# A mixture of experts in an order planned on the host: first gate products by single token blocks, one load queue at the start, and an order planned anew with shorter lengths

## The chip, the cores and the metric

The kernel runs on one core of a Trainium2 chip. The core's engines are TensorE (PE; its weight loads are listed apart as PEld), VectorE (DVE), ScalarE (ACT), GpSimd (POOL) and SyncE (SP), each with its own queue of instructions that it works off in order. The metric is the device time of one execution in microseconds (us); lower is better. All arithmetic is in float32.

## The reference

The input x has 16 batch entries of 256 tokens with 256 features. Eight routed experts and one shared expert each have an up part (two matrices of 256 x 1024, the gate G and the up matrix U) and a down matrix of 1024 x 256:

```python
g = einsum('bsd,edf->ebsf', h, Wg)
u = einsum('bsd,edf->ebsf', h, Wu)
expert_outs = einsum('ebsf,efd->ebsd', silu(g) * u, Wd)
expert_output = einsum('be,ebsd->bsd', gating_probs, expert_outs)
shared = einsum('bsf,fd->bsd', silu(h @ Sg) * (h @ Su), Sd)
x = x + (1 - sg) * expert_output + sg * shared      # h = x, sg per batch entry
```

## The kernel before

**Units.** The work is cut into 72 units: 9 experts x 2 halves of the 1024 hidden columns x 4 groups of four batch entries. A unit multiplies 512 hidden columns (four chunks of 128) with four token blocks of 256 tokens. Most units save matmuls by a fast algorithm: weights and tokens are combined at the points -1, 0, 1, 2, four diagonal products go to the one PSUM bank called D, and six pairs of points (PAIRS) give off-diagonal products in banks called M and X. The combined tokens are the tiles xd (diagonal) and xp (pairs), the combined weights wb and wp. The combined tokens of each group are made once, kept in DRAM (keep) and loaded again for later experts (load_xd, load_xp).

**Three stages.** Units 4 to 55 are "star" units: their down part also works in pairs (unit_up, unit_down), and their results are summed in DRAM as star totals. Units 1 to 3 and 56 to 71 use another form of the down part (unit_up_w, unit_down_w). At the passages between these, SBUF regions change their use (plan.shift, with the RANK entries "to" and "back"), and after unit 56 the star totals of the four groups are merged into the other totals (merge, RANK entries m0, m1, pace, ml).

**Unit 0** is computed plainly, since no combined tokens exist yet. Token blocks are loaded, transposed on TensorE (L560), and copied to SBUF by ACT (L565) as a raw pair of blocks. Eight steps (a, c), for pair a of blocks and chunk c, each have a product for the gate (m = 0, into an X bank) and one for the up matrix (m = 1, into an M bank). Each product is two matmuls of 512 columns, one for each half of the 256 features; the lower half of the weights comes from load_base, the upper half from load_raw. Before the first load lands, nine matmuls on zeros run.

**The queues of the first loads.** SP issues token block 0, block 1, the raw upper half of Wg, the lower half of Wu, then blocks 2 and 3. ACT issues two loads at the same time: the lower half of Wg and the raw upper half of Wu.

**What sets the order.** Every operation is added to a Plan with a rank, a length and a lag (HOP) until its result can be used. One rank step is a twelfth of a unit. Plan.run goes through time as these lengths say: whenever an engine is free, it takes the ready operation of the lowest rank plus "ahead" (TensorE keeps rank order in each of two streams: the dn bank's and the others), if its buffers are free. Operations of VectorE and POOL on SBUF alone (port) are booked one after another. The order that comes out is the fixed order of each engine's queue; waits between engines are by semaphore. So lengths and ranks are never executed, but decide the order. In a star unit, a diagonal goes: two matmuls into D, ACT's copy of D to a p tile (L673, rank entry "p"), two more matmuls into D, VectorE's subtraction (into pq, "q", "qa"), then ACT's SiLU of D for the gate (L874, with "ga" as its "ahead") or VectorE's product for the up part. Only then is D free for the next diagonal. ACT also scales the SiLU's result (L865) and moves down results from dn banks to ev tiles (L1103, L1026). POOL makes the differences s from p and q (L365), VectorE adds them to M to seed X (L365), and POOL combines weights. The file's helpers tt and stt record most VectorE and POOL operations, so these show lines L365 and L370; TensorE's products show L646, loads L360.

Of the kernel before, what the change touches and what calls it, by code (L numbers as in the profile page):

```python
# [16 lines left out]
P = 128  # L17
TB = 256
# [4 lines left out]


RANK = {
# [5 lines left out]
    (-15, -6, -33, -13, -49), "back": (36, 81, -9, -33, -38, 74, 23),  # L31
}


# [29 lines left out]
class Plan:  # L64
# [8 lines left out]

    HOP = 0.25
    KB = 0.0035

    def __init__(self):
# [124 lines left out]
def kernel(  # L204
# [42 lines left out]
    W = 12  # L247
# [63 lines left out]
    MM = 0.431  # L311
    TR = 0.16

    def dve(n, stt=False):
        return (0.2 if stt else 0.12) + n * 0.00112

    def act(n):
        return 0.24 + n * 0.0007

    def pool(n):  # L320
        return 0.43 + n * 0.00183 if n < 4 * P else 1.365

    ident = const.tile([P, P], F32, tag="ident", name="ident")
    make_identity(nc, ident)
# [57 lines left out]
    def load_base(m, e, half, rank, ranks=None):  # L382
        b = Buf("wb", f"wb_{m}_{e}_{half}")
        src = [
            sources(e)[m][ts(part, P), ts(half, 4 * P)].rearrange("p (c q) -> p c q", q=P)
            for part in range(2)
        ] if m < 2 else None
        late = 0 if rank < 0 else 8
        ru, rv = ranks or (rank, rank)
        if m == 2:  # L390
            rows = sources(e)[2][ts(half, 4 * P), :].rearrange("(c p) (k q) -> p c k q", p=P, q=P)
        engine = "ACT" if ranks and m == 0 else "SP"
        if m == 2:
            u = v = load(ru, lambda: b.tile, rows, 512, [], [b], late=late)
        else:
            u = load(ru, lambda: b[:, :, 0, :], src[0], 256, [], [b], late=late, engine=engine)
            v = load(rv, lambda: b[:, :, 1, :], src[1], 256, [], [], [b], late=late)
        ops = []
        for i, t in enumerate(POINTS):
            r, x_ = (lambda i=i: b[:, i, 1, :]), (lambda i=i: b[:, i, 0, :])  # L400
            if t == 0:
                op = v
            elif abs(t) == 1:
                op = tt("POOL", rank + 1, r, r, x_, ALU.add if t > 0 else ALU.subtract, P, [u, v], uses=[b])
            elif e == half == 0:
                op = stt(rank + 1, r, x_, float(t), r, ALU.add, P, [u, v], uses=[b])
            else:
                twice = Buf("wp", f"twice_{m}_{e}_{half}")
# [34 lines left out]
    def load_raw(ranks):  # L443

        b = Buf("wb", "wb_raw")
        ops = [
            load(
                ranks[m], lambda m=m: b[:, :, m, :],
                sources(0)[m][ts(1, P), 0 : 4 * P].rearrange("p (c q) -> p c q", q=P), 256,
                [], [b] if m == 0 else [], [b] if m else [], engine=("SP", "ACT")[m],  # L450
            )
            for m in range(2)
        ]
        return b, ops
# [88 lines left out]

    raw = {}

    def make_raw(a, rank, load_rank):

        b = Buf("pq", f"raw_{a}")
        done = []
        for n in range(2):  # L550
            i = 2 * a + n
            xin = Buf("xio", f"xin_0_{i}")
            src = x[i].rearrange("(h p) d -> p h d", p=P)
            ld = load(load_rank, lambda xin=xin: xin[:, :, :], src, 256, [], [xin])
            pt = Buf("dn", f"xt_0_{i}")

            def transposes(pt=pt, xin=xin):
                for k in range(2):
                    for h in range(2):
                        nc.tensor.transpose(pt[:, k, ts(h, P)], xin[:, h, ts(k, P)], ident)  # L560

            tr = add("PE", 4 * TR, rank, transposes, [ld], [pt], [xin])

            def copy(n=n, pt=pt):
                nc.scalar.copy(b[:, n : n + 3 : 2, :], pt[:, :, :])  # L565

            done.append(
                add(
                    "ACT", act(2 * TB), rank, copy, [tr],
                    [b] if n == 0 else [], [pt] if n == 0 else [pt, b],  # L570
                )
            )
        raw[a] = (b, done)
# [65 lines left out]
    def star(n):  # L639

        return FIRST <= n < LAST
# [54 lines left out]
    def offdiagonal(n, unit, k, rank, pqs, pqops, consume):  # L696

        e, half, g = unit
        i, j = PAIRS[k]
        xb, xo = xp[g, k], xpop[g, k]  # L700
        mb = Buf("M", f"M_{n}_{k}")
        m1 = []
# [8 lines left out]
        for m in range(2):  # L711
            w, wo = pair[m, e, half, k], pairop[m, e, half, k]
            p_, q_ = pqs[m]
            s, xbank = Buf("s", f"s_{m}_{n}_{k}"), Buf("X", f"X_{m}_{n}_{k}")
            so = tt(
                "POOL", rank + m - (RANK["s"] if star(n) else RANK["ws"]), lambda s=s: s[:, :, :], lambda q_=q_: q_[:, i : j + 1 : j - i, :],
                lambda p_=p_: p_[:, 3 - j : 4 - i : j - i, :], ALU.subtract, 2 * TB, [pqops[m][i], pqops[m][j]],
                [s], [p_, q_],
            )
            seed = tt(  # L720
                "DVE", rank + m + (RANK["seed"] if star(n) else RANK["wseed"]), lambda xbank=xbank: xbank[:, :, :],
                lambda m=m: mb[:, m : m + 1, :].broadcast_to([P, 2, TB]), lambda s=s: s[:, :, :], ALU.add, 2 * TB,
                [so, *m1], [xbank], [mb, s], False,
            )
            m67 = [
                mm(
                    MM, rank + m + (LAGX if star(n) else RANK["lagw"]) + (3 + h) / 8, lambda xbank=xbank, h=h: xbank[:, h, :],
                    lambda w=w, h=h: w[:, 2 - h, :], lambda h=h: xb[:, 2 - h, :],
                    False, True, True, [seed, wo, xo[2 - h]], [], [xbank, w, xb],
                )  # L730
                for h in range(2)
            ]
            consume[m](xbank, m67, rank + m + (LAGX + RANK["xc"] if star(n) else RANK["lagw"] + RANK["wxc"]), [(j, i), (i, j)])
# [35 lines left out]
    def unit_up_w(n, unit):  # L769
        e, half, g = unit  # L770
        r0 = W * n
# [39 lines left out]
        if n == 0:  # L811
            w, wops = first_raw
            readers = {0: [], 1: []}
            for step, (a, c) in enumerate((a, c) for a in range(2) for c in range(4)):
                xb, xo = raw[a]
                for m in range(2):
# [4 lines left out]
                    def view(k, xb=xb):  # L821
                        return xb.tile[:, 2 * k : 2 * k + 2, :]

                    m0 = mm(
                        2 * MM, r, lambda bank=bank: bank[:, :, :], lambda b0=b0, c=c: b0[:, c, 0, :],
                        lambda view=view: view(0), True, False, False, [u, *xo], [bank], [b0, xb],
# [5 lines left out]
                    readers[a].append(m1)  # L832
                    (gate, mult)[m](f"p{step}")(bank, [m1], r + 0.6, [(c, 2 * a), (c, 2 * a + 1)])
            for a in range(2):
                sum_raw(a, 8 + a, readers[a])
            return hb, hops

        pqs = {m: (Buf("pq", f"p_{m}_{n}"), Buf("pq", f"q_{m}_{n}")) for m in range(2)}
# [14 lines left out]
    def unit_up(n, unit):  # L853
# [7 lines left out]

        def scale(b, h, block, rank, deps):
            return add(
                "ACT", act(TB), rank,
                lambda: nc.scalar.mul(b[:, h, :], b[:, h, :], coef[:, e, 4 * g + block : 4 * g + block + 1]),  # L865
                [*deps, coef_op], uses=[b],
            )
# [475 lines left out]
    for n, unit in enumerate(units):  # L1343
        e, half, g = unit
        r0 = W * n
        if n == 0:
            make_raw(0, -14, -20)
            load_base(0, e, half, -16, (-20, -16))
            first_raw = load_raw((-19, -17.5))
            load_base(1, e, half, -15, (-18, -15))  # L1350
            make_raw(1, -5.5, -17)
        elif g == 0:
            for m in range(2):
                load_base(m, e, half, r0 - W + 3 * m - 8)
# [11 lines left out]
            rows = load_rows(e, half, r0 - 2)  # L1366
        if n == 1:
            for a in range(2):
                make_xd(g, a, -3.4 + 2 * a, -14, -3 + 2 * a)
            for k in range(len(PAIRS)):  # L1370
                make_xp(g, k, 5 + k)
            for a in range(2):
                make_xd(2, a, 3.2 + 2 * a, -13, 5 + 2 * a)
            for k in range(len(PAIRS)):
                make_xp(2, k, 11 + k / 2, True)
        elif n == 3:
            for a in range(2):
                make_xd(g, a, r0 - W + 6 * a - 4, r0 - W + 6 * a - 6, r0 - W + 6 * a - 7)
            for k in range(len(PAIRS)):
                make_xp(g, k, r0 + 2 * k - 5)  # L1380
        elif n == 4:
            for a in range(2):
                load_xd(g, a, r0 - W + 6 * a - 4)
# [101 lines left out]
```

## Time and profile before

| What | Value |
|---|---|
| Median of 3 runs | 2498.42 us (2497.76 to 2498.76) |
| The profiled execution | 2496.74 us |
| Its span, first to last instruction | 2495.0 us |
| Instructions | 34958 |
| TensorE's granted clock | 1.00 |
| DMA | 525.09 MB, mean 210 GB/s |
| VectorE 512 columns, X from M and s | 693 ns each, 632 times |
| POOL 512 columns, s from pq and pq | 1352 ns each, 852 times |
| ACT scaling of 256 columns (L865) | 509 ns each, 832 times |
| ACT eviction of a dn bank (L1103) to ev | 588 ns each, 456 times |

How to read it: a row of a group gives the line, the engine, the operation, the tile it writes and those it reads, the shape, how often, and then the busy time, the mean duration and the idle time of the engine just before. Durations are from start to end; the next operation of the same engine may start before the end of the last, so that a row's mean is longer than what one costs in a row of many. A matmul in float32 appears as two records. Times in the timeline count from the start of the span.

### The profile page before, as it was taken

The numbers are of one execution on the slowest core, as the hardware profiler recorded it, in microseconds if no ns is written. First come the engines' busy times: TensorE is split into PE (matmuls) and PEld (weight loads), VectorE is DVE, ScalarE is ACT, GpSimd is POOL, SyncE is SP. The second block draws the span as 40 slices with busy tenths as digits, with TensorE's granted clock in tenths as the row PEclk, the third lists the DMA queues.
The fourth block names the chain that finished last, engine by engine and source line by source line (L and its number), as shares of the span: only waits on it lengthen the run. The fifth ranks groups of instructions, "written<-read, shape, count | busy, mean of one in ns | idle before, by whom it ended". The sixth has DMA issues, their size and how long they took to land.

```text
span 2495.0 us, 34958 instructions
## 1 busy us (share of the span) xinstructions
PE 2473.5 (99%) x10886; PEld 2052.9 (82%) x10886; DVE 1867.7 (75%) x3142; ACT 1622.1 (65%) x3373; POOL 1807.4 (72%) x1947
## 2 busy tenths in 40 slices
PE   9999999999999999999999999999999999999999
PEld 5768888888888888888888888888888777777777
DVE  5787777777777777777777777777777888887787
ACT  3357777777777777787777778777777333333331
POOL 6777776768686868677776868586866788677764
PEclk9999999999999999999999999999999999999999
DMA  7546679888898888889988889888888888687776
GB/s 252 177 144 213 226 209 225 207 215 212 221 219 216 210 205 219 209 220 215 224 206 216 209 222 217 214 210 204 217 209 224 247 213 201 189 188 217 168 205 206
DMA packets 195770, 525.09 MB, mean 210 GB/s; under 512 B 16864, under 2 KB 83440, under 8 KB 186112
## 3 DMA queue, kind: packets, MB, share of 16 engines
q0 software_dynamic: 39552, 214.52, 44.6%
q1 hardware_dynamic: 154976, 307.81, 36.8%
q8 instruction: 87, 1.43, 0.2%
q14 instruction: 99, 0.81, 0.1%
q10 hardware_dynamic: 1056, 0.52, 0.1%
HBM read 290.53 MB, written 232.26 MB: 210 GB/s over the span
## 4 chain that ended last, share of the span: by engine, by line
PE 96%; DVE 2%; issue 1%; ACT 1%; DMA 0%; DVEq 0%; SPq 0%; ACTq 0%
PE dn L646 31%; PE M L646 22%; PE X L646 22%; PE D L646 19%; DVE h L365 1%; DVE X L365 0%; DVE pq L365 0%; PE dn L1291 0%; DVE big L370 0%; DVE h L370 0%; PE dn L522 0%; DMA side<-in_x_dram 0%; ACT sg L874 0%; DVE big L365 0%; ACT ev L1103 0%
## 5 line engine op out<-in xcount | busy, mean ns | idle before, releaser
L365 POOL TENSOR_TENSOR s<-pq,pq 128x512 f32<-128x512 f32 x852 | 1134.6, 1352 | 463.5 <-DVE X L365 233.8
L365 DVE TENSOR_TENSOR X<-M,s 128x512 f32<-128x512 f32 x632 | 427.1, 693 | 189.3 <-PE M L646 122.6
L646 PE MATMUL M<-xp,wp 128*128 128x256 f32 x1992 | 512.0, 379 | 1.9 <-DVE M L365 1.9
L646 PE MATMUL X<-xp,wp 128*128 128x256 f32 x1944 | 507.6, 379 | 1.5 <-DVE X L365 1.4
L646 PEld LDWEIGHTS M<-xp,wp 128*128 128x128 f32 x1992 | 378.1, 190 | 79.9 <-issue 25.6
L646 PE MATMUL D<-xd,wb 128*128 128x256 f32 x1696 | 436.9, 380 | 6.7 <-ACT sg L786 4.0
L646 PEld LDWEIGHTS X<-xp,wp 128*128 128x128 f32 x1944 | 368.8, 190 | 88.0 <-issue 34.8
L865 ACT ACTIVATE sg<-sg,coef 128x256 f32<-128x256 f32 x832 | 391.3, 509 | 1.2
L646 PEld LDWEIGHTS D<-xd,wb 128*128 128x128 f32 x1696 | 320.8, 190 | 75.0 <-issue 18.6
L1103 ACT COPY ev<-dn 128x512 f32<-128x512 f32 x456 | 267.4, 588 | 160.6 <-PE dn L646 157.2
L365 DVE TENSOR_TENSOR X<-X,sg 128x512 f32<-128x512 f32 x242 | 168.4, 696 | 172.1 <-ACT sg L865 109.1
L901 DVE TENSOR_TENSOR big<-big,X 128x1024 f32<-128x1024 f32 x242 | 292.6, 1209 | 0.0
L365 DVE TENSOR_TENSOR pq<-D,pq 128x256 f32<-128x256 f32 x568 | 229.4, 416 | 77.3 <-PE D L646 73.0
L646 PE MATMUL dn<-h,wp 128*128 128x256 f32 x1036 | 272.7, 379 | 0.3 <-ACT ev L1103 0.3
L673 ACT COPY pq<-D 128x512 f32<-128x512 f32 x284 | 166.5, 586 | 131.5 <-PE D L646 124.6
L646 PEld LDWEIGHTS dn<-h,wp 128*128 128x128 f32 x1036 | 196.6, 190 | 28.5 <-ACT ev L1103 0.7
L646 PE MATMUL dn<-h,low 128*128 128x512 f32 (+1 forms) x522 | 211.6, 507 | 0.0
L365 DVE TENSOR_TENSOR M<-M,s 128x512 f32<-128x512 f32 x220 | 152.5, 693 | 64.7 <-PE M L646 38.3
L1103 ACT COPY big<-dn 128x512 f32<-128x512 f32 x220 | 129.2, 587 | 77.5 <-PE dn L646 75.8
L874 ACT ACTIVATE sg<-X 128x512 f32<-128x512 f32 x224 | 134.1, 599 | 68.6 <-PE X L646 65.5
L1026 ACT COPY ev<-dn 128x512 f32<-128x512 f32 x122 | 71.4, 587 | 161.1 <-PE dn L646 159.5
L1117 POOL DMA_DIRECT2D star<-ev x130 | 113.6, 874 | 65.2 <-ACT ev L1103 51.4
(171 smaller groups left out, 3955.8 us busy)
## 6 DMA issues: line engine op xcount, KB each, us to landing
xp<-keep_p SPq DMA_DIRECT2D x408, 384.0 KB, 5.1
star<-ev POOLq DMA_DIRECT2D x104, 768.0 KB, 7.5
xd<-keep_d SPq DMA_DIRECT2D x136, 512.0 KB, 3.9
star<-big POOLq DMA_DIRECT2D x52, 768.0 KB, 7.6
star<-ev POOLq DMA_DIRECT2D x36, 1024.0 KB, 11.6
total<-ev POOLq DMA_DIRECT2D x17, 1024.0 KB, 8.6
star<-big POOLq DMA_DIRECT2D x16, 1024.0 KB, 11.3
total<-ev POOLq DMA_DIRECT2D x18, 768.0 KB, 7.6
```

The lines of the kernel that those rows point to most:

```text
L365: return add(engine, length, rank, lambda: eng.tensor_tensor(o(), a(), b(), op), deps, new, uses, port=port)
L646: lambda: nc.tensor.matmul(o(), w(), mv(), start=start, stop=stop, skip_group_check=onto),
L673: lambda: nc.scalar.copy(p_[:, 2 - 2 * a : 4 - 2 * a, :], bank[:, :, :]), ps,
L865: lambda: nc.scalar.mul(b[:, h, :], b[:, h, :], coef[:, e, 4 * g + block : 4 * g + block + 1]),
L874: lambda: nc.scalar.activation(b[:, :, :], bank[:, :, :], AF.Silu), deps, [b], [bank],
L901: "DVE", dve(4 * TB), rank, lambda: nc.vector.tensor_tensor(view(), view(), twice(), ALU.add),
L1026: lambda ev=ev, at=at, bank=bank: nc.scalar.copy(ev[:, at, :], bank.tile.rearrange("p a t -> p (a t)")),
L1103: lambda ev=ev, at=at, bank=bank: nc.scalar.copy(ev[:, at, :], bank.tile.rearrange("p a t -> p (a t)")),
L1117: nc.gpsimd.dma_start(star_total[g][part], ev[:, 0:k, :], accum_op=ALU.add)
```

## The change

Three things change in the program, and with them the order of nearly everything.

**Unit 0's first gate products.** For m = 0 and steps 0 and 1, the two matmuls of 512 columns become four of 256: first both halves of the features for block 0 (h = 0), then the same for block 1 (h = 1). Their ranks are -7 + h/5 + step/20. Each block's product depends on that block's copy alone. make_raw takes a rank for each block; block 1's transposes go to -6.97, between the two steps' products for block 0.

**One load queue at first.** The two loads issued by ACT go to SP. SP's order is then block 0, lower Wg, raw upper Wg, block 1, lower Wu, raw upper Wu, blocks 2 and 3, and the rest.

**Lengths and ranks.** The plan's lengths for VectorE, ACT and POOL become shorter, HOP longer (0.3 for 0.25); POOL's s operation in star units keeps 1.365, and the scaling by ACT is given 0.44 for 0.42. Most entries of RANK have new values, and seven ranks that were numbers in the code become entries (hX, hA, hR, hD, hE, hF, hG).

```diff
-    "first": 4, "q": 2.85, "dc": 2.95, "acc": 3.05, "g": -5.35, "cp": 1.1, "seed": -0.8, "s": 0.75,
-    "lagx": 1.0, "sc": 16.6, "bank": (6.6, 7.1, 8.6, 15.9, 16.4, 16.9, 17.3), "ev": 0.3, "p": 0.3, "xc":
-    0.2, "st": 1.7, "qa": -2.0, "da": -1.5, "ga": -4.75, "pace": 4, "m0": 0.4, "m1": 3.25, "xm": 0, "w":
-    16, "mp": 4, "m2": 1.5, "ml": 2.75, "lagw": 1.25, "wp": -0.2, "wq": 0.35, "wqa": -2.5, "wdc": 0.7,
-    "ws": 1.5, "wseed": 0.2, "wxc": 1.2, "pa": -3.5, "hd": (), "ph": 7.0, "pd": 0.75, "xh": 5.25, "to":
-    (-15, -6, -33, -13, -49), "back": (36, 81, -9, -33, -38, 74, 23),
+    "first": 4, "q": 2.85, "dc": 2.45, "acc": 2.55, "g": -5.35, "cp": 1.85, "seed": -0.3, "s": 0.75,
+    "lagx": 1.0, "sc": 15.85, "bank": (6.6, 7.1, 8.6, 15.9, 16.4, 16.9, 17.3), "ev": 0.3, "p": 2.3,
+    "xc": 0.2, "st": 1.2, "qa": -2.0, "da": -1.25, "ga": -7.25, "pace": 2, "m0": 1.9, "m1": 2.5, "xm":
+    0, "w": 16, "mp": 4, "m2": 1.5, "ml": 1.75, "lagw": 1.0, "wp": -0.95, "wq": -0.9, "wqa": -2.25,
+    "wdc": 2.2, "ws": 0.5, "wseed": 0.2, "wxc": 0.95, "pa": -4.25, "hd": (), "ph": 7.25, "pd": 1.0,
+    "xh": 5, "hX": 4.5, "hA": 10.5, "hR": 5.0, "hD": -6.5, "hE": 5, "hF": -7.75, "hG": -3.75, "to":
+    (-18, -3, -9, -16, -46), "back": (-27, 120, 21, -15, -5, 80, 20),
...
-    HOP = 0.25
+    HOP = 0.3
...
-        return (0.2 if stt else 0.12) + n * 0.00112
+        return (0.15 if stt else 0.09) + n * 0.00106
...
-        return 0.24 + n * 0.0007
+        return 0.21 + n * 0.000625
...
-        return 0.43 + n * 0.00183 if n < 4 * P else 1.365
+        return 0.38 + n * 0.00188 if n < 4 * P else 1.28
...
-        engine = "ACT" if ranks and m == 0 else "SP"
...
-                [], [b] if m == 0 else [], [b] if m else [], engine=("SP", "ACT")[m],
+                [], [b] if m == 0 else [], [b] if m else [],
...
+            if star(n):
+                so.length = 1.365
...
+                    if m == 0 and step < 2:
+
+                        m1 = None
+                        for h in range(2):
+                            rh = -7 + h / 5 + step / 20
+                            for k, (wv, wo) in enumerate(
+                                ((lambda b0=b0, c=c: b0[:, c, 0, :], u), (lambda c=c: w[:, c, 0, :], wops[0]))
+                            ):
+                                m1 = mm(
+                                    MM, rh + k / 100, lambda bank=bank, h=h: bank[:, h, :], wv,
+                                    lambda xb=xb, k=k, h=h: xb.tile[:, 2 * k + h, :], h == k == 0, k == 1, h == 1,
+                                    [wo, xo[h], m1], [bank] if h == k == 0 else [],
+                                    [w if k else b0, xb] if h == k == 0 else [w if k else b0, xb, bank],
+                                )
+                        readers[a].append(m1)
+                        gate(f"p{step}")(bank, [m1], r + 0.6, [(c, 2 * a), (c, 2 * a + 1)])
+                        continue
...
-                sum_raw(a, 8 + a, readers[a])
+                sum_raw(a, RANK["hR"] + a, readers[a])
...
-                "ACT", act(TB), rank,
+                "ACT", 0.44, rank,
...
-            make_raw(0, -14, -20)
-            load_base(0, e, half, -16, (-20, -16))
-            first_raw = load_raw((-19, -17.5))
+            make_raw(0, (-14, -6.97), (-20, -18.6))
+            load_base(0, e, half, -16, (-19, -16))
+            first_raw = load_raw((-18.8, -17.5))
             load_base(1, e, half, -15, (-18, -15))
-            make_raw(1, -5.5, -17)
+            make_raw(1, (-5.5, -5.5), (-17, -17))
...
-                make_xd(g, a, -3.4 + 2 * a, -14, -3 + 2 * a)
+                make_xd(g, a, -3.4 + 2 * a, -14, RANK["hD"] + 2 * a)
...
-                make_xp(g, k, 5 + k)
+                make_xp(g, k, RANK["hX"] + k)
...
-                make_xp(2, k, 11 + k / 2, True)
+                make_xp(2, k, RANK["hA"] + k / 2, True)
...
-                make_xd(g, a, r0 - W + 6 * a - 4, r0 - W + 6 * a - 6, r0 - W + 6 * a - 7)
+                make_xd(g, a, r0 - W + 6 * a - 4, r0 - W + 6 * a - 6, r0 - W + 6 * a + RANK["hF"])
...
-                make_xp(g, k, r0 + 2 * k - 5)
+                make_xp(g, k, r0 + 2 * k + RANK["hG"])
```

More of the change, by code (lines that the diff above doesn't have):

```diff
@@ L395, in load_base @@
         else:
-            u = load(ru, lambda: b[:, :, 0, :], src[0], 256, [], [b], late=late, engine=engine)
+            u = load(ru, lambda: b[:, :, 0, :], src[0], 256, [], [b], late=late)
             v = load(rv, lambda: b[:, :, 1, :], src[1], 256, [], [], [b], late=late)
@@ L544, with make_raw @@
     raw = {}
-    def make_raw(a, rank, load_rank):
+    def make_raw(a, ranks, load_ranks):
         b = Buf("pq", f"raw_{a}")
@@ L553, in make_raw @@
             src = x[i].rearrange("(h p) d -> p h d", p=P)
-            ld = load(load_rank, lambda xin=xin: xin[:, :, :], src, 256, [], [xin])
+            rank = ranks[n]
+            ld = load(load_ranks[n], lambda xin=xin: xin[:, :, :], src, 256, [], [xin])
             pt = Buf("dn", f"xt_0_{i}")
@@ L1368 @@
             for a in range(2):
-                make_xd(g, a, -3.4 + 2 * a, -14, -3 + 2 * a)
+                make_xd(g, a, -3.4 + 2 * a, -14, RANK["hD"] + 2 * a)
             for k in range(len(PAIRS)):
-                make_xp(g, k, 5 + k)
+                make_xp(g, k, RANK["hX"] + k)
             for a in range(2):
-                make_xd(2, a, 3.2 + 2 * a, -13, 5 + 2 * a)
+                make_xd(2, a, 3.2 + 2 * a, -13, RANK["hE"] + 2 * a)
             for k in range(len(PAIRS)):
-                make_xp(2, k, 11 + k / 2, True)
+                make_xp(2, k, RANK["hA"] + k / 2, True)
         elif n == 3:
             for a in range(2):
-                make_xd(g, a, r0 - W + 6 * a - 4, r0 - W + 6 * a - 6, r0 - W + 6 * a - 7)
+                make_xd(g, a, r0 - W + 6 * a - 4, r0 - W + 6 * a - 6, r0 - W + 6 * a + RANK["hF"])
             for k in range(len(PAIRS)):
-                make_xp(g, k, r0 + 2 * k - 5)
+                make_xp(g, k, r0 + 2 * k + RANK["hG"])
         elif n == 4:
```

## The prediction, made before the result was known

> **What bounds the kernel now.** I read the page first: busy shares and the chain that ended last.
>
> ```profile
> PE 2473.5 (99%) x10886; PEld 2052.9 (82%) x10886; DVE 1867.7 (75%) x3142; ACT 1622.1 (65%) x3373; POOL 1807.4 (72%) x1947
> PE 96%; DVE 2%; issue 1%; ACT 1%; DMA 0%; DVEq 0%; SPq 0%; ACTq 0%
> ```
>
> TensorE works 2473.5 of 2495.0 us and carries 96% of the chain. The change adds and removes no column of any product, so it can only move the other 21.5 us. Next, the busy time by stage, TensorE alone (start:end, length, PE busy, granted clock, DMA share, GB/s).
>
> ```profile
> 0.00:62.00 62.00, 56.69 (x194) 1.00 0.77 253
> 125.00:187.00 62.00, 58.59 (x218) 1.00 0.40 145
> 187.00:1875.00 1688.00, 1685.51 (x7796) 1.00 0.86 214
> 1875.00:2062.00 187.00, 182.60 (x757) 1.00 0.87 229
> 2062.00:2312.00 250.00, 249.78 (x955) 1.00 0.78 199
> 2312.00:2496.00 184.00, 177.35 (x720) 1.00 0.71 191
> ```
>
> The idle time sits where stages change: 5.3 us in the first 62, 3.4 around the passage to the star units, 2.5 in all 1688 us of star units, 4.4 at the passage out of them, 6.6 at the end, of which some 4 is the tail after the last product (it ends at 2490.8). Then who ended TensorE's waits (total, times, longest).
>
> ```profile
> PE D L646 <- ACT sg L786: 4.1, 4, 2.2
> PE D L646 <- ACT sg L874: 2.5, 8, 0.3
> PE M L646 <- DVE M L365: 1.9, 1, 1.9
> PE X L646 <- DVE X L365: 1.4, 2, 0.9
> PE dn L646 <- ACT ev L1026: 1.2, 1, 1.2
> ```
>
> These are waits for other engines, not for loads. A 256-column matmul is drawn 0.38 long but the next starts 0.216 later, so each stall is some 0.16 larger than its idle time. The list's 26 waits sum to 17.1; 26 x 0.16 makes it about 21, and without the 1.2 before the very first matmul about 20. **That is the ceiling**: 20 us, 0.8%.
>
> **The start.** The timeline of the first 11 us:
>
> ```profile
> 0.74 0.48 ACTq L360 DMA_DIRECT2D wb<-in_L_cond_Wg_dram  x1
> 0.74 0.95 SPq L360 DMA_DIRECT2D side<-in_x_dram  x2
> 5.43 0.59 ACT L565 COPY pq<-dn 128x512 f32<-128x512 f32 x1 [2.68 <-PE dn L560]
> 6.51 0.66 PE L560 MATMUL dn<-ident,side 128*128 128x128 f32 x4 [1.12 <-DMA side<-in_x_dram]
> 7.21 0.59 ACT L565 COPY pq<-dn 128x512 f32<-128x512 f32 x1 [1.19 <-PE dn L560]
> 7.85 2.25 PE L646 MATMUL X<-pq,wb 128*128 128x512 f32 x4 [0.68 <-ACT pq L565]
> ```
>
> Block 0 of the tokens is copied by 6.02; TensorE then stands until block 1 lands (about 6.5) and again until its copy ends at 7.80. From start to start these two stalls are 1.27 and 0.83 us, and 0.25 and 0.14 more go where X and M wait for weights. The change puts first the gate products of steps 0 and 1 on block 0 alone: 2 steps x 2 halves of the contraction x 0.431 = 1.73 us. A 512-column product is two records of 0.431, a 256-column one two of 0.216, so splitting adds no TensorE time; the 4 further products need 8 further weight loads, 0.19 each, which lie under matmuls (D products, which change weights every 0.216 us, run without a gap), and 1.5 us if they did not. The first can start when the copy is done, 6.02 + 0.05 (7.80 to 7.85 now) = 6.07. It needs the first Wg load (landed 5.67) and the raw Wg load, which the change moves ahead of block 1. The landings now are 4.63, 5.67, 6.47, 7.29, 8.92, 10.03 for six loads of 256 KB; if loads keep these slots in the new order (x0, Wg, raw Wg, x1, Wu, raw Wu), raw Wg is there at 6.47, x1 at 7.29. Then: step 0 until 6.95, block 1's transposes and step 1 in either order until about 8.3, the second halves until 10.0 to 10.6, where now only step 0's X has been done by 9.98. The lead is 1.1 to 1.7 us; I take **1.5**.
>
> The two ACT loads go to SP: 0.48 + 0.47 us of issue stand ahead of block 1 and of what follows it (blocks 2 and 3, both upper halves of the weights, the eight x loads of the next groups). ACT's queue is freed of them, but ACT idles until 5.43 anyway. Here the Trainium skill ("DMA: Bandwidth & Descriptors", "Issuing engines are not separate DMA queues") holds that issuing from several engines saves only issue time: by it the move costs at most 0.95 us of issue, hidden because SP's fifth load is issued at 2.25 and lands at 10.03. The trace is less kind: with both queues at work 4 to 6.5 us move near 300 GB/s, but between 7.3 and 8.4, after ACT's two are done, the rate falls to 86 to 160. By the row, one queue could cost one landing slot, 0.8 to 1.6 us, most of the lead; I keep 1.5 and put a lead of zero into the range.
>
> Whether the lead survives is decided near 51 to 60 us: stalls of 0.41, 1.07 and 1.33 us, where D waits for ACT's copy, X for its seed and dn for an eviction. There POOL, which began at 12.6, is the loaded engine; work that waits for it does not come earlier because TensorE does. I credit half a microsecond for the new order there (bounds: 2.8 gained, 1.5 lost again).
>
> **The shorter lengths.** They enter the order only; no instruction becomes faster. From start to start, back to back, the chip takes 0.598 us for a 512-column VectorE operation on PSUM, 0.331 for 256, 0.48 on ACT for 512, 1.23 on POOL. The old plan assumes 0.693, 0.407, 0.598 and 1.365, the new one 0.633, 0.361, 0.53 and 1.28 (1.365 kept in star units); the hand-over grows from 0.25 to 0.3. So it is still on the safe side and nearer. What that is worth is visible in the star units:
>
> ```profile
> 1015.36 0.59 ACT L1103 COPY big<-dn 128x512 f32<-128x512 f32 x1 [0.71 <-PE dn L646]
> 1015.59 0.59 PE L646 MATMUL dn<-low,wp 128*128 128x256 f32 x2
> 1015.84 0.60 ACT L874 ACTIVATE sg<-D 128x512 f32<-128x512 f32 x1
> 1016.50 0.70 PE L646 MATMUL D<-xd,wb 128*128 128x256 f32 x2 [0.31 <-ACT sg L874]
> ```
>
> The D bank was complete at 15.04 (VectorE's subtraction), but ACT, in its fixed order, stood 0.71 us before an eviction that was listed ahead of the gate; the single D bank came free late, and D starts at 16.50, not 15.59 + 2 x 0.216 = 16.02: 0.48. This happens 8 times: 3.8 us. The change raises the gate's priority ("ga" from -4.75 to -7.25) and plans the subtraction shorter; both favour the gate. All 8 repaired gives 3.8, none 0, new ones elsewhere a loss; I take **2.4**, the greater part.
>
> Against the lengths speaks the skill's "SBUF — State Buffer", "Who interferes with whom": a VectorE operation with two SBUF inputs is blocked while a GpSimd operation reads SBUF. The plan books one port in turn; the chip does worse:
>
> ```profile
> 1973.38 4.91 DVE L365 TENSOR_TENSOR h<-h,h 128x512 f32<-128x512 f32 x1
> 1976.73 1.00 POOL L365 TENSOR_TENSOR wp<-wp,wb 128x256 f32<-128x256 f32 x1
> ```
>
> An operation of 0.69 took 4.91 because POOL ran seven operations in a row, the last of them this one. The D subtraction, ACT's gate and the D bank came late behind it, and TensorE lost 2.3 us at 1980. By the rule as worded, one POOL operation (1.3) would be the price; by the row it is several. The same stands behind the 0.97 at 2016, 0.33 at 2205 and 1.17 at 2344. Shorter lengths do not cure this, so outside the star units I credit the re-ranked order little: 0.8 of 4.0 us at 125 to 187 (moved "to" points, group sums and pair sums), 0.5 of 5.4 at 1875 to 2062 (merges at 1.9 + 2.5k units instead of 0.4 + 3.25k, four ranks apart before, two now), 0.3 of 2.3 after that. Each can as well be 4 better or 4 worse. The "p" rank, 0.3 to 2.3, lets ACT's copy of D (L673) yield to other work. It now starts 0.09 us after the product and ends 0.89 before the next D product (median; 0.45 in the tightest tenth). One operation of 0.48 in front costs 0.03 in that tenth, two 0.07 at the median, 15 us if all 52 x 4 = 208 copies of the star units stood so; ACT is idle for 22% of these units, so I cost it at nothing and leave it to the range. The later keeps and loads of xd and xp move with these ranks on SP; TensorE waited for no load after 97 us, so they cost nothing unless late by several us.
>
> **Sum.** 1.5 + 0.5 + 0.8 + 2.4 + 0.5 + 0.3 = 6.0 us off the span: 2489.0. The profiled execution took 2496.74, 1.74 more than its span, so 2490.7; the runs' median, 2498.42, lies 1.68 above that execution: **2492.4**.
>
> **Rivals.** *Absorbed:* the start's lead is lost at 51 to 60 and the re-ranked passages trade old stalls for new; saving 0 to 5, about 2496.5. For it: the waits at the passages have about ten different releasers. Against: the 8 equal stalls have one cause, which the change addresses. *Slower, by lock-outs:* the merges' steps now follow two ranks apart instead of four and VectorE's operations on two SBUF tiles stand denser among POOL's; every one that is shut out like the one at 1973 delays the D subtraction behind it and costs up to 2.33. Five more of them between 1875 and 2496 are 11.7, less the 6.0: 2504.1; from the fifth on the result is slower by over 0.2%. For it: thirteen VectorE operations on SBUF tiles, ten of them after 1970, already take over 1.3 us longer than their like, and the plan's port does not know it. Against: only five of these cost TensorE anything, 5.0 us together; the others lie under work that it has. *Better:* all 8 gates and most of the passages repaired, 12 to 16 saved, 2484.
>
> **Chances.** Forecast with its better end 50%, absorbed 28%, slower 22%. Two tenths of a per cent, 5.0 us, is what a measurement here can tell from no change. The range runs from 2484 (4% below it) to 2505 (some 14% above).
>
> **What would show it.** Right: X records of 256 columns at about 6.1, no stall over 0.7 before 10 us; the row of D waiting for L874 gone or under 3 times; the star stage above 1687 busy. Wrong: D waiting for L673 in the star units, a VectorE operation of 3 us or more near 1900 to 2100 with D waiting behind it, or TensorE waiting for a weight load in the first 12 us.

## The result and the profile after

The changed kernel takes **2484.49 us**, the median of 6 runs (2481.36 to 2485.36), where the kernel before takes 2498.62 in the same series (6 runs, 2497.76 to 2499.61): a ratio of 0.9941, 95% interval 0.9929 to 0.9954. It is 14.1 us faster; the forecast was 6.0. The profiled execution went from 2496.74 to 2482.88, its span from 2495.0 to 2480.8.

Busy time of each engine, and the shares of the chain that ended last, in the profile after:

```profile
PE 2469.3 (100%) x10894; PEld 2055.7 (83%) x10894; DVE 1857.2 (75%) x3142; ACT 1606.0 (65%) x3373; POOL 1807.2 (73%) x1947
PE 99%; ACT 1%; DMA 0%; DVE 0%; issue 0%; SPq 0%; DVEq 0%
```

TensorE has the same products to do, and 11.5 us of its own span are left in which it does none. VectorE's 2% of the chain are gone. TensorE by stage (start:end, length, PE busy, granted clock, DMA share, GB/s):

```profile
0.00:62.00 62.00, 56.68 (x205) 1.00 0.77 254
125.00:187.00 62.00, 61.66 (x235) 1.00 0.44 160
187.00:1875.00 1688.00, 1686.50 (x7803) 1.00 0.85 214
1875.00:2062.00 187.00, 186.84 (x767) 1.00 0.83 220
2062.00:2312.00 250.00, 250.00 (x960) 1.00 0.82 212
2312.00:2470.00 158.00, 158.00 (x640) 1.00 0.66 186
```

Against the same rows of before, the first 62 us are no busier (5.3 us idle, as before), although this is where the change does most by hand. The passage at 125 to 187 has 0.34 us of idle time where it had 3.41, the passage at 1875 to 2062 has 0.16 where it had 4.40. Who ended TensorE's waits (total, times, longest):

```profile
PE X L647 <- DMA wb<-in_L_cond_Wg_dram: 3.0, 1, 3.0
PE X L354 <- DVE zero L327: 1.2, 1, 1.2
PE X L647 <- ACT pq L566: 0.9, 2, 0.7
PE D L647 <- ACT sg L894: 0.8, 2, 0.4
PE dn L647 <- ACT ev L1123: 0.4, 1, 0.4
```

The 26 waits of before are nine now. The long ones for ACT's gate at the passages and for VectorE's merges have gone, and there is one that did not exist: 3.0 us for a load of the gate weights.

Idle time understates a stall, as the prediction says, so the loss was also counted from the starts of the matmuls: what lies between two starts beyond the usual step (0.216 us after a record of 256 columns, 0.431 after 512, 0.119 after 128). Summed by stage, in us:

```
                        0-50  50-200  200-1900  1900-2050  2050-end     sum
before                  2.00    7.55      5.32       5.99      1.62   22.48
after                   3.71    1.00      3.98       0.64     -1.03    8.30
gained                 -1.71    6.55      1.34       5.35      2.65   14.18
forecast                1.5      1.3       2.4        0.5       0.3     6.0
```

(The sums carry an offset: the last stage can come out negative, and with exactly 0.216 as the step the star stage, 200 to 1900, comes out 2.0 lower in both kernels; records of 128 columns are in fact 0.109 apart. So only differences between kernels are used.) The 14.18 agrees with the 14.2 between the two spans. Three stages that the prediction credited with 2.1 us together, all after the first 50 us and outside the star units, gave 14.55; the start and the star units, credited with 3.9, gave -0.37.

### The profile page after: what moved, and what is told of

Same layout as the page of the kernel before. It is cut to its first block, busy times and chain, and to the rows that moved or that the text cites. A ratio compares the mean times of both kernels' runs of the same rounds, so it can differ in the third digit from the quotient of the medians.

```text
span 2480.8 us, 35084 instructions
## 1 busy us (share of the span) xinstructions
PE 2469.3 (100%) x10894; PEld 2055.7 (83%) x10894; DVE 1857.2 (75%) x3142; ACT 1606.0 (65%) x3373; POOL 1807.2 (73%) x1947
## 4 chain that ended last, share of the span: by engine, by line
PE 99%; ACT 1%; DMA 0%; DVE 0%; issue 0%; SPq 0%; DVEq 0%
PE dn L647 33%; PE X L647 25%; PE M L647 20%; PE D L647 20%; DMA wb<-in_L_cond_Wg_dram 0%; PE dn L1311 0%; ACT sg L894 0%; PE dn L522 0%; ACT sg L885 0%; PE dn L561 0%; ACT wp L438 0%; SPq L361 0%; DVE X L366 0%; DVEq L1500 0%; ACT pq L674 0%
## 5 line engine op out<-in xcount | busy, mean ns | idle before, releaser
L366 POOL TENSOR_TENSOR s<-pq,pq 128x512 f32<-128x512 f32 x852 | 1116.0, 1337 | 450.0 <-DVE X L366 347.1
L366 DVE TENSOR_TENSOR X<-M,s 128x512 f32<-128x512 f32 x697 | 466.8, 692 | 155.7 <-PE M L647 98.9
L647 PE MATMUL X<-xp,wp 128*128 128x256 f32 x2204 | 570.2, 379 | 0.0
L647 PEld LDWEIGHTS X<-xp,wp 128*128 128x128 f32 x2204 | 418.4, 190 | 82.8 <-issue 24.6
L647 PE MATMUL D<-xd,wb 128*128 128x256 f32 x1760 | 454.6, 380 | 1.4 <-ACT sg L894 0.8
L647 PE MATMUL M<-xp,wp 128*128 128x256 f32 x1732 | 448.3, 379 | 0.3 <-DVE X L366 0.3
L647 PEld LDWEIGHTS M<-xp,wp 128*128 128x128 f32 x1732 | 328.8, 190 | 70.6 <-issue 23.2
L647 PE MATMUL dn<-h,low 128*128 128x512 f32 (+1 forms) x498 | 199.0, 503 | 0.0
L366 DVE TENSOR_TENSOR low<-X,h 128x256 f32<-128x256 f32 x233 | 97.5, 419 | 94.2 <-ACT h L969 93.8
L647 PE MATMUL M<-xp,low 128*128 128x256 f32 x592 | 157.5, 379 | 0.0
## 6 DMA issues: line engine op xcount, KB each, us to landing
star<-big POOLq DMA_DIRECT2D x18, 1024.0 KB, 11.3
```

What stands on the lines that cost most here:

```text
L366: return add(engine, length, rank, lambda: eng.tensor_tensor(o(), a(), b(), op), deps, new, uses, port=port)
L647: lambda: nc.tensor.matmul(o(), w(), mv(), start=start, stop=stop, skip_group_check=onto),
```

## The experiments

All were timed beside the kernel before; its median was 2499.95 us in the first series (the two mends of the start one by one, the lengths alone, the ranks alone), 2498.50 in the second (both mends, the old start, the old merge and the old gate ranks) and 2498.43 in the third (the rest). Losses are those of the table's method.

### The late load: one queue, or what shares it

The timeline of the changed kernel's start shows the new wait:

```profile
1.23 1.01 SPq L361 DMA_DIRECT2D wb<-in_L_cond_Wg_dram  x2
5.25 0.59 ACT L566 COPY pq<-dn 128x512 f32<-128x512 f32 x1 [3.01 <-PE dn L561]
5.89 0.70 PE L647 MATMUL X<-pq,wb 128*128 128x256 f32 x2 [0.67 <-ACT pq L566]
9.55 1.13 PE L647 MATMUL X<-pq,wb 128*128 128x256 f32 x4 [2.97 <-DMA wb<-in_L_cond_Wg_dram]
```

The first line is the issue of the two gate loads, base and raw. TensorE starts the first gate product on 256 columns at 5.89, does the matmul on the base weights (two records), and then stands 2.97 us until the raw gate weights land at 9.51. In the prediction they land at 6.47. The rate of the DMA engines in slices of 0.35 us from 0 to 14 us, after the change:

```profile
GB/s 0 0 0 0 0 47 82 339 367 338 243 171 114 167 199 120 102 69 61 51 208 301 329 328 347 359 361 350 303 322 332 287 268 338 291 279 315 246 332 320
q1 hardware_dynamic: 4599, 2.97, 71.6%
q0 software_dynamic: 64, 0.07, 11.3%
```

From about 3.5 to 7 us the rate falls from 243 to 51. In that time the packets of POOL's queue (q0: the two broadcasts of the probabilities, 64 and 8 KB) are in flight: 16 of 4 KB, 16 of 512 bytes and 32 of 4 bytes. Twelve of them take 1.0 to 1.7 us, where most packets of SP's queue take 0.03 to 0.05, and from 6.0 to 7.0 us 9 to 15 of them are in flight at once. They carry 0.07 MB and take 11.3% of the engines' time. Two theories. Q: a single load queue can't keep the engines filled past these packets, two can. B: the broadcasts hold the engines, and whatever is then still to be moved is late.

**Two queues again**, all else as after:

```diff
-def load(rank, dst, src, kb, ..., engine="SP"):
-    queue = {"SP": nc.sync, "ACT": nc.scalar}[engine]
+def load(rank, dst, src, kb, ..., engine="SP", issue=None):
+    queue = {"SP": nc.sync, "ACT": nc.scalar}[issue or engine]
...
+# lower Wg block and raw Wu: issue="ACT"; the planned order stays
```

> The changed kernel with its whole order kept, but the lower half of Wg and the raw upper half of Wu issued by ACT again. In the changed kernel TensorE waits 2.97 us at 6.6 for the raw upper half of Wg, which lands at 9.51. Theory Q (the single queue makes that load late): it lands near 6.5 to 7, the wait falls under 0.8 and the time by 2 to 2.5 us against the changed kernel's 2484.5. Theory B (the two small broadcast loads of POOL hold the 16 DMA engines from about 5 to 7.5 us, whatever queue the large loads use): it still lands after 8.5, the wait stays above 2 us, the time within 1 us.

Measured: 2480.88 us (2479.86 to 2482.01), ratio 0.9926 (0.9914 to 0.9939). The raw weights land at 6.31 and the wait is gone. B's forecast for this kernel fails.

**The broadcasts later**, one queue kept:

```diff
-nc.gpsimd.dma_start(p_bc..., probs...broadcast_to([P, B * E]))
-nc.gpsimd.dma_start(coef[:, E, :], shared_prob...broadcast_to([P, B]))
+def broadcasts():            # the same two, by nc.sync
...
+    if op is first_raw[1][1]:
+        broadcasts()
+        make_coef()
     op.emit()
```

> The changed kernel with its order kept and one load queue, but POOL's two broadcast loads (routing weights and shared gate) are issued by SP after the lower half of Wu, and the coefficients are made from them then. Theory B: the raw upper half of Wg lands near 6 to 6.5, the wait of 2.97 falls under 0.5, the time by 2 to 3 us to about 2482. Theory Q: that load still lands after 8.5, the wait stays above 2 us and the time within 1 us of 2484.5.

Measured: 2481.15 us (2480.80 to 2481.29), ratio 0.9927 (0.9914 to 0.9941). The raw weights land at 6.30. Q's forecast fails here. TensorE's timeline of this kernel:

```profile
5.90 1.58 PE L649 MATMUL X<-pq,wb 128*128 128x256 f32 x6 [0.68 <-ACT pq L568]
7.31 0.60 PE L563 MATMUL dn<-ident,side 128*128 128x128 f32 x4
```

This is the start that the prediction describes: products from 5.90 on, block 1's transposes behind them, no stall between. The rate falls in this kernel too, to 16 to 26 GB/s between 7.35 and 8.4 us, but no product waits for a load then.

**Both together:**

```diff
+# issue="ACT" for the two loads, and broadcasts() by nc.sync, as above
```

> The changed kernel with its order kept and both mends of the start: lower half of Wg and raw upper half of Wu issued by ACT, and the two broadcast loads issued by SP after the lower half of Wu. If either mend already removes the whole wait (theory B or Q, one cause seen from two sides), nothing is added: 2480.5 to 2481.5, the second block's copy as the next limit. If the two are separate delays, another microsecond comes off: 2479.5 to 2480.

Measured: 2480.84 us (2480.74 to 2481.00), ratio 0.9927 (0.9915 to 0.994). Neither adds to the other: both mends take away the same wait. With two queues the broadcasts' first packet starts at 5.64 us instead of 3.80, and those of 512 bytes from 6.87 on, when the load has landed (6.31). So the load is late where it is still to be moved when the broadcasts' packets fill the engines, and each mend puts it ahead of them. Why the second queue holds the broadcasts back is not shown, and the other mend changes two things at once, the time of the broadcasts and the queue that issues them.

The three kernels gain 3.3 to 3.6 us on the changed one by their medians (of different series, in which before differs by up to 1.3), but 1.6 (2482.88 to 2481.29) by the profiled executions of after and of the later broadcasts. After's runs spread over 4.0 us, those with the later broadcasts over 0.5. So the price of the wait varies from run to run. The four profiles of kernels with this start show a likely reason: the wait is 3.0 us in after, 2.2, 2.0 and 1.2 with the old merge ranks, the ranks alone and the old gate ranks (all below), but in these three TensorE's clock is at half behind it, until 14.6, 11.7 and 13.7 us, and the first 50 us lose 5.5, 4.5 and 5.2 instead of 3.7. With one profile for each kernel this is not shown to be what spreads after's runs.

### What is the split itself worth?

The first products whole, the load ranks and queues of before, all other ranks and lengths of after:

```diff
-if m == 0 and step < 2:
-    ...                       # products by halves of 256 columns
-    continue
-make_raw(0, (-14, -6.97), (-20, -18.6))
-load_base(0, e, half, -16, (-19, -16))
-first_raw = load_raw((-18.8, -17.5))
+make_raw(0, (-14, -14), (-20, -20))
+load_base(0, e, half, -16, (-20, -16))
+first_raw = load_raw((-19, -17.5))
+# lower Wg and raw Wu from ACT's queue again
```

> The changed kernel with the first products, load ranks and queues of before; new lengths and ranks stay, the order is planned anew. Theory S (the split is worth what I costed, 1.1 to 1.7 us, and the single queue took more than that away): start stalls of 2.0 to 2.5 us as before, all else as in the changed kernel, about 2482.5: 1.5 slower than with the split on two queues (2480.9), 2 faster than the changed kernel. Theory N (the split is worth nothing, the lead is lost later): 2481.

Measured: 2480.99 us (2480.93 to 2481.76), ratio 0.9929 (0.9916 to 0.9941): the same as 2480.88 with the split on two queues. Its waits:

```profile
PE X L648 <- ACT pq L567: 0.7, 1, 0.7
PE dn L562 <- DMA side<-in_x_dram: 0.5, 1, 0.5
PE M L648 <- DMA wb<-in_L_cond_Wu_dram: 0.4, 1, 0.4
```

It does lose more in the first 50 us than the undisturbed split, 1.93 against 1.31, but 0.6 us of lead do not reach the end: 1900 to 2050 loses 0.63 against 1.21, and the tail after the last product is 4.51 against 4.88. Also, 1.93 is about what before loses there. So the split is worth nothing measurable, and the start as changed costs some 3.5 us, all of it through the late load.

### Lengths and ranks

Where do the 14.55 come from? L: from the plan's shorter lengths and longer hop, whatever the ranks. R: from the new ranks. I: only from both, since ranks are chosen for a plan.

**The lengths alone**, on the kernel before:

```diff
-HOP = 0.25
+HOP = 0.3
-    return (0.2 if stt else 0.12) + n * 0.00112
+    return (0.15 if stt else 0.09) + n * 0.00106
-    return 0.24 + n * 0.0007
+    return 0.21 + n * 0.000625
-    return 0.43 + n * 0.00183 if n < 4 * P else 1.365
+    return 0.38 + n * 0.00188 if n < 4 * P else 1.28
...
+# so.length = 1.365 in star units, 0.44 in scale, as in the change
```

> The kernel before with the new lengths and hand-over alone: ranks, first products and queues are those of before. Theory L (the truer lengths make the better order): the 18 us of stalls after the first 16 us fall under 8, the time to 2486 to 2490. Theory R (the new ranks do it): within 3 us of 2498.6. Theory I (ranks belong to the lengths they were chosen with, and only the pair is good): as slow as before or slower, 2498 to 2510.

Measured: 2489.87 us (2489.69 to 2491.12), ratio 0.9964 (0.9952 to 0.9977): 10.1 us of the 14.1. Two of its stages:

```profile
125.00:187.00 62.00, 60.79 (x233) 1.00 0.45 164
1875.00:2062.00 187.00, 183.44 (x750) 1.00 0.85 234
```

The first passage is mended (50 to 200: 7.55 lost before, 1.98 now), the second hardly (5.99 before, 5.35 now). L's time holds, but it expected under 8 us of losses; they are 14.2 after the first 50.

**The ranks alone**: after with the old lengths.

```diff
+# HOP, dve, act, pool and scale of before; so.length removed
```

> The changed kernel with the old lengths and hand-over: new ranks, first products and one queue stay. Theory R: within 2 us of 2484.5. Theory L: most of the gain is gone, 2493 to 2500. Theory I: the gain is gone and more, 2496 to 2510, with stalls at both passages. Its first 12 us are as in the changed kernel in all three (wait for the raw Wg load about 3 us).

Measured: 2502.57 us (2499.6 to 2504.24), ratio 1.0013 (1.0004 to 1.0021), slower than before.

```profile
125.00:187.00 62.00, 59.08 (x218) 1.00 0.40 148
1875.00:2062.00 187.00, 186.49 (x771) 1.00 0.85 222
2312.00:2470.00 158.00, 153.66 (x593) 0.98 0.70 193
```

The reverse: the second passage is mended (1.23 lost), the first is worse than ever (9.52 from 50 to 200), and the end loses 11.66; stretches at half clock behind two stalls, 3.41 and 6.83 us long, make up some 1.7 and 3.4 of these two losses. Lengths and ranks each mend one passage; the ranks alone gain nothing. This kernel also has the late load of the changed start, some 3.5 us by the runs above; without it, it would be about as fast as before.

**The old merge ranks and give-back times**, on after:

```diff
-"pace": 2, "m0": 1.9, "m1": 2.5, "ml": 1.75, "back": (-27, 120, 21, -15, -5, 80, 20),
+"pace": 4, "m0": 0.4, "m1": 3.25, "ml": 2.75, "back": (36, 81, -9, -33, -38, 74, 23),
```

> The changed kernel with m0, m1, pace, ml and back as before, all else new. Theory M (merges and regions given back at other times make the passage out of the star units smooth): stalls between 1900 and 2062 grow from 0.6 to 4 or 6 us, time 2488 to 2491. Theory O (other ranks of the last units do it): they stay under 1.5, time within 1.5 us of 2484.5.

Measured: 2493.51 us (2492.97 to 2494.4), ratio 0.9981 (0.9972 to 0.9989), 9.0 slower than after by the medians; 8.92 are lost between 1900 and 2050, more than theory M gave. The stage, and two waits of the whole kernel:

```profile
1875.00:2062.00 187.00, 181.47 (x735) 1.00 0.86 229
...
PE dn L639 <- DVE h L358: 2.1, 3, 1.3
PE X L639 <- DVE X L358: 1.8, 2, 1.5
```

These merge ranks and give-back times together are what mends the second passage (which of them was not separated): the prediction credited "merges at 1.9 + 2.5k units" with 0.5.

**The old gate and copy ranks**, on after:

```diff
-"p": 2.3, "ga": -7.25,
+"p": 0.3, "ga": -4.75,
```

> The changed kernel with ga (-4.75) and p (0.3) as before. Theory G (the gate's priority removes the eight equal stalls of D in the star units): D waits for L894 8 times or more, stalls of the star stage 4 to 6 us against 4.0 with the change, time 2485 to 2487. Theory H (ga and p matter little, the lengths decide): star stalls within 1 us of 4.0, time within 1 us of 2484.5.

Measured: 2483.97 us (2482.16 to 2484.99), ratio 0.9939 (0.9926 to 0.9953); star units lose 4.10 where after loses 3.98. With the new lengths, the two ranks are worth nothing measurable; the prediction had paid 2.4 for "ga" and the shorter subtraction.

### Which lengths, and is it their truth?

Three kernels take one engine's lengths on the kernel before, two of them with the new HOP; the fourth moves all the other way.

**VectorE's:**

```diff
-HOP = 0.25
+HOP = 0.3
-    return (0.2 if stt else 0.12) + n * 0.00112
+    return (0.15 if stt else 0.09) + n * 0.00106
```

> The kernel before with the new hand-over and VectorE's new lengths only (512 columns: 0.633 for 0.693 with 0.3 for 0.25 behind it, so that a result is still expected after 0.93 and only the engine is free sooner). All new lengths together gave 2489.9. Theory V (the passages are limited by VectorE's booking): most of that gain, 2489 to 2492, stalls between 50 and 200 us 2 to 3 instead of 7.5. Theory S (the set of lengths must fit together): under 4 us of gain or a loss.

Measured: 2502.02 us (2497.66 to 2505.08), ratio 1.0014 (1.0004 to 1.0024): 3.6 slower, with 6.27 still lost from 50 to 200: theory S.

**ScalarE's:**

```diff
-HOP = 0.25
+HOP = 0.3
-    return 0.24 + n * 0.0007
+    return 0.21 + n * 0.000625
+# and 0.44 in scale
```

> The kernel before with the new hand-over and ACT's new lengths only. ACT has most room in both passages (33% busy before 62 us and after 1940). Theory V: less than 3 us of gain, stalls between 50 and 200 us above 5. Theory A (ACT's evictions and gates are what come late): 2490 to 2493. Theory S: under 4 us of gain or a loss.

Measured: 2491.62 us (2491.18 to 2492.09), ratio 0.9975 (0.9964 to 0.9985): 6.8 faster, within what theory A gave, but 50 to 200 still loses 5.64. In the profiles all losses together fall by 3.7 and the tail by 0.6; that is most of the 4.7 between the two profiled executions (2496.74 and 2492.09), of which before's is a fast one of its kind.

**GpSimd's:**

```diff
-    return 0.43 + n * 0.00183 if n < 4 * P else 1.365
+    return 0.38 + n * 0.00188 if n < 4 * P else 1.28
+# so.length = 1.365 in star units
```

> The kernel before with POOL's new lengths only (512 columns 1.28 for 1.365 outside the star units; hand-over as before). Theory P (POOL's booking decides where VectorE's operations on two SBUF tiles are put, and so the lock-outs): half the gain or more, 2488 to 2494, and fewer VectorE operations over 1.3 us too long after 1970 than the ten of before. Theory V: less than 3 us of gain.

Measured: 2495.99 us (2492.91 to 2497.95), ratio 0.999 (0.9981 to 1.0): hardly to be told from before, with eight VectorE operations after 1970 us that take over 1.3 us too long, where before has ten. Theory P fails.

**All longer:**

```diff
-HOP = 0.25
+HOP = 0.2
-    return (0.2 if stt else 0.12) + n * 0.00112
+    return (0.25 if stt else 0.15) + n * 0.00118
-    return 0.24 + n * 0.0007
+    return 0.27 + n * 0.000775
-    return 0.43 + n * 0.00183 if n < 4 * P else 1.365
+    return 0.48 + n * 0.00178 if n < 4 * P else 1.45
```

> The kernel before with all lengths moved by about the same step the other way (VectorE 512 columns 0.754, ACT 0.667, POOL 1.45, hand-over 0.2), further from what the chip takes. Theory L (truer lengths give better orders): 2502 to 2512. Theory C (any other lengths shuffle the order, and before was merely a poor draw): 2485 to 2500.

Measured: 2512.75 us (2511.04 to 2513.03), ratio 1.0056 (1.0041 to 1.0071). One of its stages:

```profile
2062.00:2312.00 250.00, 245.37 (x931) 0.99 0.75 196
```

In before, this stage has 0.22 us of idle time, here 4.63. Star units lose 10.48, the end 13.16. So for the whole set the sign goes with the lengths: longer is 14 us slower, shorter 10 faster. But +3.6, -6.8 and -2.4 for the single engines don't make -10.1 by any mechanism seen here (HOP, which is in two of them, was never moved alone): every length gives another order of the whole kernel. What is shown is the whole set; which length in it matters, and through which order, stays open, and two sets that go the right way do not rule out chance, so that it is the truth of the lengths is not shown.

## Why the prediction was wrong

**Direction, bound and ceiling** held. TensorE was the bound and stayed it, and "20 us" of recoverable time was about right: 14.2 came, and some 6 to 8 are left (the offset of the count is 2). 2484.49 us is nearly the "Better" rival's 2484, but that rival's mechanism, "all 8 gates and most of the passages repaired", is half right: the passages, not the gates.

**The step that failed** is: "Shorter lengths do not cure this, so outside the star units I credit the re-ranked order little". Its terms 0.5, 0.8, 0.5 and 0.3 measured 6.55 (50 to 200), 5.35 (1900 to 2050) and 2.65 (after that). The premise is true: after still has eleven VectorE operations that take over 1.3 us too long, ten of them after 1970 us, where before had thirteen and ten. The conclusion doesn't follow. Their number does not even decide: the kernel with the old merge ranks has five, and loses more at the second passage than any other kernel here. Two lines from the kernel with the old merge ranks, and two from after:

```profile
2005.42 4.15 DVE L358 TENSOR_TENSOR h<-h,h 128x512 f32<-128x512 f32 x2
2007.99 0.70 PE L639 MATMUL dn<-h,low 128*128 128x512 f32 x1 [1.25 <-DVE h L358]
```

```profile
2196.36 4.28 DVE L366 TENSOR_TENSOR big<-h,h 128x512 f32<-128x512 f32 x2
2197.21 1.03 PE L647 MATMUL M<-xp,wp 128*128 128x256 f32 x4
```

The same kind of pair takes as long in both. In the first, the product needs the result of the first operation and waits. In the second, TensorE runs on (no wait in brackets) since the order has other products there. The prediction itself said of the lock-outs of before that "only five of these cost TensorE anything"; the order decides which do. It asked whether the cause goes away, where the question was whether anyone waits behind it. The lengths do most of this in the first passage (they save 5.6 there with the old ranks), the merge ranks and give-back times in the second; only both together mend both.

**The start** was forecast at +1.5 and measured -1.71 (2.00 lost before, 3.71 after). The step is "if loads keep these slots in the new order ... raw Wg is there at 6.47". Those slots were the landings of two queues; on one, the third load landed at 9.51. The bound "by the row, one queue could cost one landing slot, 0.8 to 1.6 us" was the right worry and too small: the slip is 3.04. Its ground was misread too: the fall to 86 to 160 GB/s is not what one queue can do, since one queue moves above 330 from 5.3 to 6.3 us in the kernel with the later broadcasts; before's broadcast packets of 512 bytes are in flight from 6.7 to 9.4 us, around that fall. The rule that the prediction took from the Trainium skill ("DMA: Bandwidth & Descriptors", "Issuing engines are not separate DMA queues"), that issuing from several engines saves only issue time, is contradicted while the broadcasts come from POOL: with the order kept, two queues land this load 3.20 us earlier and the runs are 3.6 us shorter. With the broadcasts later it agrees: 2481.15 us on one queue, 2480.84 on two. The prediction's own sign of error, TensorE waiting for weights in the first 12 us, is what appeared. And with the stall mended, the lead of the split is 0.6 and doesn't reach the end.

**The star gates** were forecast at 2.4 and the stage gave 1.34. The 8 equal stalls went, but new ones came, before the D products at 1230.1, 1366.1, 1501.2, 1636.7 and 1771.8, of the same kind. After's timeline at the third:

```profile
1500.52 0.59 ACT L894 ACTIVATE sg<-D 128x512 f32<-128x512 f32 x1
1501.16 1.13 PE L647 MATMUL D<-xd,wb 128*128 128x256 f32 x4
```

The D bank is again given back by a gate that ran late (0.31 lost). Since the old "ga" and "p" measure the same, the 1.34 comes from the rest of the order, not from the rank that raises the gate. The step that failed here is "both favour the gate", of the raised rank and the shorter subtraction: the kernel with the ranks alone has no stall of D behind the gate in the star units and loses 3.2 us less there than before, most of the 3.8, so it is with the new lengths that such stalls come back. Which rank removed the eight was not tried.

**"p" costed at nothing** held: in the star units ACT's copy of D starts a median 0.09 us after its product, at worst 1.86, and nothing waits for it. **Keeps and loads moved on SP** cost nothing, as said: no wait for a load after the first.

The best kernels of the study are the changed one with either mend of its start, 2480.84 to 2481.15 us: some 3.5 us below the change and 17.7 below before (both mends against 2498.50).

## What to carry to other kernels

Where a planner writes the order, don't price a change of its lengths or ranks by asking whether it removes the cause of a stall: count how much of the bounding engine's loss sits where the order is free to move, and take all of it as open in both directions (here 22.5 us of loss became 8.3, 16.5, 29 or 39 with other lengths and ranks). Landing times read off two load queues don't hold for one: before taking a queue away, look for small transfers that hold the DMA engines when the next load is due. Then time the hand-made part by itself, since the gain of the whole hid a part that costs 3.5 us.

## What the runs showed of the hardware

Two broadcasts of 72 KB together, issued by POOL, had 9 to 15 packets in flight on the 16 DMA engines from 6.0 to 7.0 us, the longest 1.7 us, and the rate went from above 330 to 51 GB/s, with 256 KB loads waiting in the other queue.

TensorE's clock was halved behind stalls that are not long. In the kernel with the ranks alone (the end of a stall, then start:end, length, PE busy, granted clock, DMA share, GB/s):

```profile
59.71 1.65 PE L647 MATMUL X<-xp,wp 128*128 128x256 f32 x3 [2.45 <-DVE X L366]
60.00:64.00 4.00, 4.00 (x12) 0.63 0.53 180
2400.00:2404.00 4.00, 4.00 (x13) 0.50 0.22 50
```

This stall of 2.45 us, and one of 3.05 that ends at 2398.3, came with half clock for 3.41 and 6.83 us. The Trainium skill ("TensorE: Matmul & The Clock Gate", Part 1, "What's actually happening") has free-running windows of 3413 ns, which these lengths agree with. It has the throttle come after an idle window of some 3.4 us, while 2.45 was enough here; the 2.97 of the changed kernel's profile, and a stall of 3.17 us at 176 with VectorE's lengths alone, were followed by no half clock.

The clock's first rise differs too. The same four transposes of block 0, in after and with two queues again:

```profile
4.61 0.60 PE L561 MATMUL dn<-ident,side 128*128 128x128 f32 x4
5.01 1.06 PE L561 MATMUL dn<-ident,side 128*128 128x128 f32 x4
```

In after, the steps between matmuls shorten at about 4.2 us; with two queues again only at 10.6, with matmuls of 256 columns 0.43 apart until then instead of 0.216, although the matmuls on zeros start at 1.20 us in both. So a stall can cost more than its own length, by half of what then runs at half clock (some 1.7 and 3.4 us here), and differently from run to run.
